# Moving four rings of buffers by a few words inside SBUF: start addresses modulo 256 bytes in a TensorE-bound MoE kernel

## The chip, the cores and the metric

The kernel runs on one NeuronCore of a Trainium2 chip. The metric is the device time of one execution in microseconds (us). Five engines work beside each other and meet at semaphores: PE (TensorE, the matrix engine), DVE (VectorE), ACT (ScalarE), POOL (GpSimd) and SP (SyncE, which here only issues DMAs). They share SBUF, an on-chip memory of 128 partitions; an address below is always a byte offset inside a partition, the same in all 128. Matmul results land in PSUM.

A matmul on PE has two operands in SBUF. The *stationary* one (128 columns here) is loaded into the array by a LDWEIGHTS instruction; the *moving* one (448 or 256 columns here, called rows below[...]) then streams through it. In the profile "PEld" is the row of weight loads and "PE" the row of matmuls; a weight load can run while the matmul before it still streams. The *pitch* of a matmul is the time from its start to the start of the next matmul.

## The reference

One layer: cross-attention over 16 batches of 112 tokens (width 256, context of 375), then a mixture of 8 experts of which every token uses all, weighted by a router.

```python
x = x + xattn(layernorm(x), ctx_1024, Wq, bq, Wk, bk, Wv, bv)
# ffn, on hidden = layernorm(x), 16*112 = 1792 tokens, H = 256, F = 1024, E = 8
g = einsum('bsh,ehf->ebsf', hidden, w_gate)
u = einsum('bsh,ehf->ebsf', hidden, w_up)
h = silu(g) * u
expert_out = einsum('ebsf,efh->ebsh', h, w_down)
out = einsum('ebsh,bse->bsh', expert_out, cw)     # cw: product of two softmaxes, normalised
x = x + out
```

All inputs and outputs are float32.

## The kernel before

**Attention first.** Up to about 110 us the attention of the 16 batches runs, a generator per batch advanced by a hand-written order (`tick`), and its tail is mixed into the first two steps of the expert loop. Its matrix products are plain float32, except the output projection `ps_o` (L337), which multiplies split operands like the expert loop does.

**The expert loop.** `steps` (L435) counts 8 experts x 2 halves of the tokens x 4 blocks of 256 hidden units x {gate, up} = 128 steps. Every float32 operand is split into a high and a low part of type float32r, and a product is three matmuls: high x high, high x low, low x high (`PASSES`, L79). One step computes a 256 x 256 by 256 x 896 product by Strassen-Winograd's seven products instead of eight (`PROD`, L20). `prod` (L568) does one of the seven: three matmuls, stationary a 128-column slice of the split gate or up weights `w` (high or low), moving a 448-column tile `xs_hi` or `xs_lo` of the prepared tokens (L573). A step has 21 of these.

Between them `fill` (L589) interleaves the down projection of earlier steps. `down_group` (L526) is three matmuls into a PSUM accumulator `pd` (L539): stationary a 128-token slice of `hhi` (twice) or `hlo` (once), the two parts of silu(gate) x up, moving the 256-column split down weights `wd` (high, low, high). There are 2688 matmuls of L573 and 2688 of L539, and the order on PE is the one written out in `step` (L646): runs of three, six or nine matmuls of the one kind and then of the other.

**What the other engines do for it.** ACT makes the high parts (`load_hi` L481, `load_d` L490, `keep_hidden` L625), POOL subtracts to make the low parts of the weights (`load_lo` L486, L491), DVE combines the seven products out of PSUM and makes `hlo` (L626, L633). SP issues the DMAs of raw weights.

**Where the buffers lie.** Buffers that rotate come from one pool, `fpool`, through one helper, `buf(tag, ...)` (L103); a tag is a ring with the number of buffers in `BUFS` (L101). The pool lays its rings one behind the other, in the order in which their tags first appear in the program, each buffer after the last: `y`, `w`, `d` (down weights), `rawd`, `hhi`, `hlo`, `tt`, `s`, `v1`, `raw`. Behind them comes the pool of small tiles. The tiles of another pool, the constants (`xs_hi`, `xs_lo`, the accumulators), lie ahead. As built, every buffer of `fpool` has a size that is a multiple of 256 bytes, so a whole ring has one remainder modulo 256. These are the remainders at which tiles begin:

| tiles | role on PE | bytes of a buffer | begins at, modulo 256 |
|---|---|---|---|
| `xs_hi`, `xs_lo` | moving, L573 | 1792 | 192 |
| `w` (gate and up, high and low) | stationary, L573 | 7168 | 64 |
| `d` (`wd`, high and low) | moving, L539 | 4096 | 64 |
| `hhi`, `hlo` | stationary, L539 | 3584 | 64 |
| `rawd`, `tt`, `s`, `v1`, `raw` | not read by PE in the loop | 2048 or 1792 | 64 |

A slice inside these (a product's weights, 128 tokens, the low half) is a multiple of 512 bytes from the tile's start, so it has the tile's remainder.

Of the kernel before, what the change touches and what calls it, by code (L numbers as in the profile page):

```python
# [8 lines left out]
F32 = mybir.dt.float32  # L9
# [22 lines left out]
def kernel(  # L32
# [18 lines left out]
    P = 128  # L51
# [20 lines left out]
    fpool = ctx.enter_context(tc.tile_pool(name="ffn", bufs=2))  # L72
# [27 lines left out]

    BUFS = {"w": 8, "d": 4, "hhi": 4, "hlo": 4, "s": 11, "v1": 2, "raw": 3, "rawd": 2, "tt": 2, "y": 3}  # L101

    def buf(tag, shape, name, dtype=F32):  # L103
        return fpool.tile(shape, dtype, tag=tag, name=name, bufs=BUFS[tag])

    zero = buf("y", [P, 256], "zero")
    nc.vector.memset(zero, 0.0)
    zero = zero.bitcast(mybir.dt.bfloat16)
# [16 lines left out]

    WF = 2 * 7 * P
    wide = [buf("w", [P, WF], f"wide{i}") for i in range(7)]
    qk_b = [wide[0][:, i * KC * GT : (i + 1) * KC * GT] for i in range(2)]
    late = [wide[i] for i in (3, 1, 2)]
# [4 lines left out]
    x1T = [wide[5 + h].rearrange("p (k t) -> p k t", k=KC) for h in range(NH)]  # L134

    wn = buf("d", [P, 2, KC, D], "wn")
    wT = buf("d", [P, 2, KC, D], "wT")
    wv_b = buf("d", [P, 2, KC, D], "wv_b", FR)
# [768 lines left out]
```

## Time and profile before

| | |
|---|---|
| median of 3 runs | 1004.95 us (1004.35 to 1006.24) |
| the profiled execution, its own time | 1002.7 us |
| its span, first to last instruction | 1000.9 us |
| granted TensorE clock, mean | 0.988 |
| DVE busy | 802.8 us (80%) |
| ACT busy | 496.4 us (50%) |
| POOL busy | 419.0 us (42%) |
| DMA queue of SP | 37.76 MB, 13.1% of 16 engines' span |

The profiled execution took 1.8 us more than its span, and 2.3 us less than the median of the runs. "Busy" is time in which at least one instruction of the engine is recorded. A matmul's recorded duration reaches over the start of the next ones, because they are pipelined and their ends are modelled; the distances between starts tell the rate at which PE moves.

### The profile page before, as it was taken

The numbers are of one execution on the slowest core, as the hardware profiler recorded it, in microseconds if no ns is written. First come the engines' busy times: TensorE is split into PE (matmuls) and PEld (weight loads), VectorE is DVE, ScalarE is ACT, GpSimd is POOL, SyncE is SP. The second block draws the span as 40 slices with busy tenths as digits, with TensorE's granted clock in tenths as the row PEclk, the third lists the DMA queues.
The fourth block names the chain that finished last, engine by engine and source line by source line (L and its number), as shares of the span: only waits on it lengthen the run. The fifth ranks groups of instructions, "written<-read, shape, count | busy, mean of one in ns | idle before, by whom it ended". The sixth has DMA issues, their size and how long they took to land.

```text
span 1000.9 us, 16367 instructions
## 1 busy us (share of the span) xinstructions
PE 980.1 (98%) x6052; PEld 911.3 (91%) x6052; DVE 802.8 (80%) x1529; ACT 496.4 (50%) x1036; POOL 419.0 (42%) x548
## 2 busy tenths in 40 slices
PE   8989889999999999999999999999999999999998
PEld 4868779999999999999999999999999999999998
DVE  5886668888878888878887887888887888788786
ACT  4555655445535554445544553555444544455342
POOL 2352765344605552356324460555235632455000
PEclk9999979999999999999999999999999999999999
DMA  9710111001100110011100110011001110010011
GB/s 216 213 30 16 53 32 53 16 28 44 53 1 23 43 43 22 12 42 37 39 11 22 44 54 1 22 44 43 22 11 43 44 32 11 22 43 2 1 37 38
DMA packets 36736, 39.06 MB, mean 39 GB/s; under 512 B 3552, under 2 KB 34656, under 8 KB 36656
## 3 DMA queue, kind: packets, MB, share of 16 engines
q1 hardware_dynamic: 36384, 37.76, 13.1%
q8 instruction: 47, 0.77, 0.3%
q10 hardware_dynamic: 272, 0.26, 0.1%
q14 instruction: 33, 0.27, 0.1%
HBM read 34.34 MB, written 1.84 MB: 36 GB/s over the span
## 4 chain that ended last, share of the span: by engine, by line
PE 93%; DVE 2%; DMA 2%; ACT 1%; POOL 1%; issue 0%; SPq 0%; DVEq 0%
PE pd L539 32%; PE pC L573 16%; PE pA L573 16%; PE pB L573 15%; PE pE L573 8%; PE ps_s L300 2%; PE ps_aT L327 1%; DMA wide<-in_x_dram 1%; PE ps_o L337 1%; PE ps_qk L271 1%; PE ps_lg L401 1%; DMA ctx<-in_ctx_dram 1%; PE ps_cT L293 1%; PE ps_pT L318 1%; ACT xs_hi L375 0%; POOL w L486 0%
## 5 line engine op out<-in xcount | busy, mean ns | idle before, releaser
L539 PE MATMUL pd<-wd,hhi 128*128 128x256 f32 x1792 | 338.6, 280 | 0.0
L539 PEld LDWEIGHTS pd<-wd,hhi 128*128 128x128 f32 x1792 | 310.1, 189 | 15.8
L539 PE MATMUL pd<-wd,hlo 128*128 128x256 f32 x896 | 251.9, 281 | 0.0
L573 PE MATMUL pC<-xs_hi,w 128*128 128x448 f32 x512 | 189.3, 370 | 0.8 <-DVE s_3c L702 0.8
L573 PE MATMUL pA<-xs_hi,w 128*128 128x448 f32 x512 | 188.6, 368 | 0.5 <-ACT v L674 0.4
L573 PE MATMUL pB<-xs_hi,w 128*128 128x448 f32 x512 | 187.9, 367 | 0.0
L539 PEld LDWEIGHTS pd<-wd,hlo 128*128 128x128 f32 x896 | 169.7, 189 | 0.2 <-DVE hlo L626 0.2
L556 POOL TENSOR_TENSOR acc<-acc,y 128x256 f32<-128x256 f32 x45 | 36.1, 831 | 248.4 <-ACT y L555 248.4
L486 POOL TENSOR_TENSOR w<-raw,w 128x384 fp32r<-128x384 f32 x64 | 73.0, 1141 | 136.8 <-ACT w L481 136.8
L674 ACT COPY v<-pA 128x448 f32<-128x448 f32 x128 | 68.1, 532 | 91.2 <-PE pA L573 91.2
L573 PEld LDWEIGHTS pC<-xs_hi,w 128*128 128x128 f32 x512 | 96.8, 189 | 10.0 <-DVE s_3c L702 1.1
L573 PEld LDWEIGHTS pA<-xs_hi,w 128*128 128x128 f32 x512 | 96.8, 189 | 6.0 <-ACT v L674 1.1
L573 PEld LDWEIGHTS pB<-xs_hi,w 128*128 128x128 f32 x512 | 97.2, 190 | 5.5
L573 PE MATMUL pC<-xs_lo,w 128*128 128x448 f32 x256 | 94.1, 368 | 0.0
L573 PE MATMUL pA<-xs_lo,w 128*128 128x448 f32 x256 | 94.1, 368 | 0.0
L573 PE MATMUL pE<-xs_hi,w 128*128 128x448 f32 x256 | 93.7, 366 | 0.0
L573 PE MATMUL pB<-xs_lo,w 128*128 128x448 f32 x256 | 93.3, 364 | 0.0
L486 POOL TENSOR_TENSOR w<-tt,w 128x512 fp32r<-128x512 f32 x64 | 82.9, 1296 | 2.6
L491 POOL TENSOR_TENSOR wd<-rawd,wd 128x512 fp32r<-128x512 f32 x32 | 41.8, 1307 | 72.7 <-ACT wd L490 72.7
L573 PEld LDWEIGHTS pE<-xs_hi,w 128*128 128x128 f32 x256 | 48.2, 188 | 3.9
L573 PEld LDWEIGHTS pB<-xs_lo,w 128*128 128x128 f32 x256 | 48.9, 191 | 1.9
L573 PEld LDWEIGHTS pC<-xs_lo,w 128*128 128x128 f32 x256 | 48.3, 189 | 2.3
(1779 smaller groups left out, 1884.4 us busy)
## 6 DMA issues: line engine op xcount, KB each, us to landing
raw<-in_L_ffn_w_gate_dram SPq DMA_DIRECT2D x32, 256.0 KB, 3.7
raw<-in_L_ffn_w_up_dram SPq DMA_DIRECT2D x32, 256.0 KB, 2.7
rawd<-in_L_ffn_w_down_dram SPq DMA_DIRECT2D x32, 256.0 KB, 2.8
ctx<-in_ctx_dram SPq DMA_DIRECT2D x13, 336.0 KB, 7.3
wide<-in_x_dram SPq DMA_DIRECT2D x4, 448.0 KB, 4.7
out_dram<-acc SPq DMA_DIRECT2D x6, 256.0 KB, 2.2
wide<-in_ctx_dram SPq DMA_DIRECT2D x3, 336.0 KB, 7.0
ctx<-in_ctx_dram SPq DMA_DIRECT2D x13, 39.0 KB
```

The lines of the kernel that those rows point to most:

```text
L271: nc.tensor.matmul(ps, m_sb[:, k, m * P : (m + 1) * P], xnT[:, k, :], start=(k == 0), stop=(k == KC - 1),)
L293: nc.tensor.transpose(ps[:, c * KT : (c + 1) * KT], ct[:, c, k * P : (k + 1) * P], ident[:KT, :KT])
L300: nc.tensor.matmul(sc, qkT[g][:, k, i * TQ : (i + 1) * TQ], ctT[k], start=(k == 0), stop=(k == KC - 1),)
L318: nc.tensor.transpose(ps[:, c, :], p[:, c * KT : (c + 1) * KT], ident[:TQ, :TQ])
L327: nc.tensor.matmul(ps[:, k, :], ct[:, c, k * P : (k + 1) * P], pT[:, c, :], start=(c == 0), stop=(c == NK - 1),)
L337: nc.tensor.matmul(po, aT[:, a, k, :], (wv_hi, wv_lo)[w][:, k, :], start=(k == 0 and s == 0), stop=(k == KC - 1 and s == 2),)
L486: nc.gpsimd.tensor_sub(wts[k][1][:, d], w, f(wts[k][0][:, d]))
L491: nc.gpsimd.tensor_sub(t[:, 1], rawds[q], f(t[:, 0]))
L539: nc.tensor.matmul(pd, hs[a][:, t * P : (t + 1) * P], wds[q][w][:, fi, :], start=(opening and s == 0), stop=(last and s == 2), skip_group_ ...
L556: nc.gpsimd.tensor_add(acc[tt], acc[tt], y)
L573: nc.tensor.matmul(ps, w_[w][:, wi, :], (xs_hi, xs_lo)[a][h][xi], start=(start and s == 0), stop=(stop and s == 2), skip_group_check=True,)
L674: nc.scalar.copy(v1, pa)
```

## The change

`buf` gets a second table. When one of four tags appears for the first time, a small tile of its own (16 or 32 float32 words, 64 or 128 bytes) is taken from the same pool just ahead of the ring. Nothing ever writes or reads these tiles.

```diff
     BUFS = {"w": 8, "d": 4, "hhi": 4, "hlo": 4, "s": 11, "v1": 2, "raw": 3, "rawd": 2, "tt": 2, "y": 3}
 
+
+    AHEAD = {"w": 16, "d": 32, "hhi": 16, "hlo": 32}
+
     def buf(tag, shape, name, dtype=F32):
+        if tag in AHEAD:
+            fpool.tile([P, AHEAD.pop(tag)], F32, tag=f"ahead_{tag}", name=f"ahead_{tag}", bufs=1)
         return fpool.tile(shape, dtype, tag=tag, name=name, bufs=BUFS[tag])
```

As built, this moves everything behind `y`:

| tiles | modulo 256 before | after |
|---|---|---|
| `xs_hi`, `xs_lo`, `y`, accumulators | 192, 192, 64, 192 | the same |
| `w` | 64 | 128 |
| `d`, and `rawd` behind it | 64 | 0 |
| `hhi` | 64 | 64 |
| `hlo`, and `tt`, `s`, `v1`, `raw` behind it | 64 | 192 |

In all 384 bytes per partition are taken. The instructions of each of the five engines, their order and the semaphores that they wait for are the same as before; only start addresses differ.

## The prediction

> **What bounds the kernel now.** I read the page's busy table first, then the stages, then single starts on PE.
>
> ```profile
> span 1000.9 us, 16367 instructions
> ...
> PE 980.1 (98%) x6052; PEld 911.3 (91%) x6052; DVE 802.8 (80%) x1529; ACT 496.4 (50%) x1036; POOL 419.0 (42%) x548
> ...
> PE 93%; DVE 2%; DMA 2%; ACT 1%; POOL 1%; issue 0%; SPq 0%; DVEq 0%
> ```
>
> PE carries 93% of the chain that ended last. The waits of PE, cut to the steady part of the loop (150 to 985 us), hold one row of 0.8 us, and the stages view of a part of it shows PE without a gap:
>
> ```profile
> PE pC L573 <- DVE s_3c L702: 0.8, 1, 0.8
> ```
>
> ```profile
> 500.00:900.00 400.00, 400.00 (x2490) 379.75 (x2490) 329.82 (x563) 200.21 (x395) 171.33 (x212) 1.00 0.10 29
> ```
>
> The columns are length, then busy time and count of PE, PEld, DVE, ACT, POOL, then clock, DMA share, GB/s. So the pitch of the matmuls is the time. By line the same stretch has 1248 matmuls of L539 and 1242 of L573, that is 1248 x 256 + 1242 x 448 = 875,904 rows.
>
> Now the price of a row. PE ran at half clock around 137 us; its timeline (start, recorded duration) there, then at full clock:
>
> ```profile
> 136.14 0.57 PE L573 MATMUL pA<-xs_lo,w 128*128 128x448 f32 x1
> ...
> 138.75 0.57 PE L573 MATMUL pC<-xs_hi,w 128*128 128x448 f32 x1
> ```
>
> ```profile
> 503.04 0.36 PE L573 MATMUL pA<-xs_hi,w 128*128 128x448 f32 x1
> 503.24 0.36 PE L573 MATMUL pA<-xs_lo,w 128*128 128x448 f32 x1
> 503.44 0.36 PE L573 MATMUL pA<-xs_hi,w 128*128 128x448 f32 x1
> 503.65 0.36 PE L573 MATMUL pB<-xs_hi,w 128*128 128x448 f32 x1
> ```
>
> ```profile
> 506.79 0.40 PE L539 MATMUL pd<-wd,hhi 128*128 128x256 f32 x2
> 507.03 0.28 PE L539 MATMUL pd<-wd,hlo 128*128 128x256 f32 x1
> 507.15 0.40 PE L539 MATMUL pd<-wd,hhi 128*128 128x256 f32 x2
> 507.39 0.28 PE L539 MATMUL pd<-wd,hlo 128*128 128x256 f32 x1
> 507.51 0.37 PE L573 MATMUL pB<-xs_hi,w 128*128 128x448 f32 x1
> ```
>
> At half clock seven matmuls of L573 take 2.61 us, 373 ns each: 0.833 ns a row and nothing over. A row at full clock is then 0.4165 ns, 186.6 ns for 448 and 106.6 for 256. At full clock L573 has a pitch of 203 (three in 0.61 us) and a long run of L539 of 120 (six in 0.72 us). From all single starts I get a mean of 203.1 for L573 (stalls over 230 ns left out) and 118.0 for L539. So 16.5 and 11.4 ns a matmul are neither rows nor waits, 35 us of the 400 above (875,904 x 0.4165 = 364.8), and they are gone when the rows come at half the rate. The other engines do not make them either: from step to step the same place of the loop repeats its pitch within 1 ns, though in gate steps ACT takes silu and in up steps DVE multiplies. The plain float32 matmuls of the attention, which take two clocks a row (375 rows in 315 ns, 312.5 by the count), have nearly none. I read the excess as two streams of PE meeting in SBUF: the moving rows at full rate, and the next weights, whose load starts 2 to 3 ns after each matmul and is recorded with 188 ns. The change alters where those two streams start, and nothing else.
>
> **What the Trainium skill says.** "TensorE: Matmul & The Clock Gate", section Back-to-back issue gap, prices an isolated matmul at N / 2.4 + 2.5 ns: 189.2 for 448, 109.2 for 256. The trace is 14 and 9 ns above. The same page, Step-by-step, says of the two read ports of PE that loading the next weights "doesn't steal SBUF read bandwidth from the running matmul"; the excess that is there at full clock and not at half speaks against that here. "SBUF — State Buffer", Who interferes with whom, has no contention but that of DVE with GpSimd, and Operand start alignment treats start addresses as a matter of legality and says that its runs "timed nothing". No page gives a price for a remainder modulo 256: it has to be bounded.
>
> **The change part by part.**
>
> *Instructions.* None is added, removed or moved, on no engine and no queue, SP's DMAs included. Set-up cost 0.
>
> *Which offsets change.* Take the start of the weights being loaded minus the start of the rows streaming, modulo 256, for each pair of neighbours on PE.
> - L573 behind L573 (2190 pairs): 64 - 192 = 128 before, 128 - 192 = 192 after.
> - L539 behind L539 (2190): 0 before. After: 64 for a load of `hhi` (two in each group of three, but for those that start a run: 1294), 192 for a load of `hlo` (896).
> - L539 behind L573 (498): 128 before and after. L573 behind L539 (497): 0 before, 128 after.
>
> *What an offset costs.* The loop shows only 128 (excess 16.5) and 0 (11.4; 13.3 in long runs). The one other place with split operands is `ps_o`, whose rows start at 64 and whose weights (112 columns) start at 192, 0, 0 and 128 in its second to fifth gap: offsets 128, 192, 192, 64. Over the 13 batches that ran at full clock these gaps average 115.5, 117.6, 114.6 and 117.5 ns: 116.3, or 9.7 over the rows. Weights of 112 columns are 7/8 of 128, so a full load would cost 11.1. The plain float32 scores `ps_s` have all four offsets and 314 to 315 ns at each once they run, so at half the row rate no offset costs anything.
>
> *L539.* From 11.4 to 11.1: 0.3 x 2190 = 0.7 us gained. Bounds: all excess above the skill's gap gone, 8.8 x 2190 = 19 us gained; L573's excess instead of its own, 5.1 x 2190 = 11 us lost.
>
> *L573.* If the offset is what makes it dearer, it falls from 16.5 to 11.1: 5.4 x 2190 = 11.8 us gained. If its length is, nothing. `ps_o` at offset 128 is no dearer than at the others, which speaks for length; but the same load of 128 columns should meet the same number of rows in both kinds, which speaks for offset. I take two thirds, 7.9 us. Bounds: 13.9 x 2190 = 30 us gained, and 5.4 x 2190 = 12 us lost if 192 is as much worse than 128 as 128 is than the rest.
>
> *The turns.* L539 to L573 goes from 0 to 128: at worst 5.1 x 497 = 2.5 us lost, taken as 0, as a turn at 128 in the other direction shows no jump of its own.
>
> *Other engines.* DVE, ACT and POOL read and write at new remainders. DVE's combinations (L679, L700, L702, L714, L724) take 602 to 624 ns each with all their SBUF operands at one remainder, and those with two SBUF inputs start at 610 too, so I see no price that could go or come. Cover if there were one: DVE is busy 83% of the steady part, and PE waits for it 0.8 us. Gone, that cover would cost at one place only, the wait of pC for DVE, where a few steps already start over 100 ns late (some 2 us in all). What comes due next if PE gets faster is the same wait: DVE has 400 - 330 = 70 us spare in 400, so a few per cent do not reach it.
>
> *Sum.* 0.7 + 7.9 = 8.6 us less than the profiled 1002.7: 994.1. Its distance to the median (2.3) added: 996.4, say 996.
>
> **The rivals.**
> - *Offsets do not matter, only the two rates do* (1005). For it: `ps_o` with mixed offsets costs per column of weights what L539 costs with offset 0. Against it: [...] no run of the trace holds another offset long enough.
> - *The new offsets keep the two streams in step* (slower). Rows advance at up to twice the speed of a load, so a stream that starts 64 bytes apart can run into the other and stay with it. Place: the long runs of L539, now at 64 and 192. Price: L539 at L573's excess, 5.1 x 2190 = 11 us, L573 unchanged: 1016. It decides once the mean pitch of L539 goes over 118 + 7.9 / 2.19 = 121.6 ns. For it: L573 pays 16.5 with its start apart, L539 11.4 with the same start. Against: `ps_o`.
> - *The excess mostly goes* (970): half to two thirds of the pool above the skill's gap, 30 + 19 us. For it: nothing in the records but the size of the pool.
> - *The free words do not shift what PE reads*: excluded, as the tiles' addresses are moved as the title says.
>
> **How the numbers follow.** Forecast, a gain of some 3 to 20 us: 0.42. Excess mostly gone: 0.10. No effect: 0.17. Slower: 0.31. About 0.2% (2 us) is what a measurement of this kernel tells from no change; that is 0.37 ns a matmul, so "same" holds only where offsets have no effect or the two kinds cancel. Faster 0.52, same 0.17, slower 0.31. The likeliest case alone spans 985 to 1002; the range over the cases, leaving some 0.1 at each end, is 971 to 1017.
>
> **What would show it.** Right: L573's pitch in the timeline falls from 203 to about 199 and L539's long runs stay at 117 to 120, with clock 1.00 and the wait table as it is. Offsets without effect: 203 and 120 again. The slower rival: long runs of L539 at 123 or more. I would be wrong in kind if the time moved while these two pitches stood still, for then another engine's accesses would have carried it; and wrong in part if L539 took the gain and L573 none.

## The result, and the profile after

| | before | after |
|---|---|---|
| median (lowest to highest) of 19 runs each, us | 1004.89 (1002.06 to 1006.63) | 1001.23 (999.53 to 1003.28) |
| ratio, with its 95% interval | | 0.9969 (0.9959 to 0.9978) |
| the profiled execution, span in us | 1000.9 | 1000.8 |
| loop, step 10 to step 126, in those two traces, us | 783.8 | 781.6 |

The change is worth 0.31% (0.22 to 0.41), some 3 us. The forecast was 0.9%. The two profiled executions are no guide to that: their spans agree because after's attention part, ahead of the loop, took longer in this one execution (the loop begins at 112.7 us instead of 110.2; in the traces of the kernels below that keep the whole layer it begins anywhere from 109.8 to 114.0). The same stretch of the loop is 2.2 us shorter.

The page of the kernel after, its busy table and the shares of its chain:

```profile
span 1000.8 us, 16367 instructions
...
PE 978.5 (98%) x6052; PEld 911.8 (91%) x6052; DVE 802.9 (80%) x1529; ACT 496.1 (50%) x1036; POOL 419.4 (42%) x548
...
PE 93%; DVE 2%; DMA 2%; ACT 1%; POOL 0%; issue 0%; SPq 0%; DVEq 0%
```

Its waits of PE in the steady part, 150 to 985 us (total, times, longest):

```profile
PE pC L578 <- DVE s_3c L707: 0.8, 1, 0.8
```

And 400 us of the loop (length, busy time and count of PE, PEld, DVE, ACT, POOL, clock, DMA share, GB/s):

```profile
500.00:900.00 400.00, 400.00 (x2497) 380.87 (x2496) 330.36 (x565) 199.78 (x394) 170.87 (x212) 1.00 0.10 29
```

Same instructions, same chain, same single wait of 0.8 us, full clock. PE gets through 2497 matmuls in the 400 us instead of 2490: it moves at a shorter pitch, by 0.3%, and these views show no other change. The pitch shows in the timeline of PE in the kernel after (start, recorded duration; the lines are the earlier ones plus 5, so L544 was L539 and L578 was L573):

```profile
500.10 0.36 PE L578 MATMUL pA<-xs_hi,w 128*128 128x448 f32 x1
500.30 0.36 PE L578 MATMUL pA<-xs_lo,w 128*128 128x448 f32 x1
...
501.10 0.36 PE L578 MATMUL pE<-xs_hi,w 128*128 128x448 f32 x1
501.30 0.40 PE L544 MATMUL pd<-wd,hhi 128*128 128x256 f32 x2
...
502.24 0.28 PE L544 MATMUL pd<-wd,hlo 128*128 128x256 f32 x1
502.36 0.37 PE L578 MATMUL pB<-xs_hi,w 128*128 128x448 f32 x1
...
502.98 0.40 PE L544 MATMUL pd<-wd,hhi 128*128 128x256 f32 x2
```

The six matmuls of L573 from 500.10 to 501.30 take 200 ns each. The nine of L539 from 501.30 to 502.36 take 118. The three of L573 that follow them take 207 (502.36 to 502.98): the same instruction with operands at the same remainders is 7 ns dearer here than 2 us earlier. That last reading is the one that the forecast had no place for.

All later numbers are mean pitches, worked out as here from single starts in each trace, from 150 us on, with stalls over 230 ns left out. A turn is the place where a run of one kind of matmul ends and a run of the other begins. A pitch belongs to a matmul and to the load for the next one, so there are four kinds of neighbours. In the table the offset (next weights' start minus running rows' start, modulo 256) stands in brackets. "Sum" is each difference from before, times the 2190, 497, 498 and 2190 such pairs, in us; "measured" is the ratio's distance from 1 times 1005 us. Each ratio is to the kernel before, run on the same chip in the same sitting. Lines are named as in the kernel before. The nine kernels below "after" belong to the experiments.

| kernel | L539 to L539 | L539 to L573 | L573 to L539 | L573 to L573 | sum | measured |
|---|---|---|---|---|---|---|
| before | 117.8 (0) | 118.6 (0) | 205.3 (128) | 202.5 (128) | | |
| after | 117.2 (64), 119.2 (192) | 117.4 (128) | 205.2 (128) | 200.9 (192) | -3.6 | -3.1 |
| w_only | 118.2 (0) | 117.9 (64) | 202.8 (128) | 202.1 (192) | -1.8 | -1.8 |
| d_only | 115.9 (64) | 116.6 (64) | 202.8 (128) | 203.7 (128) | -3.9 | -4.9 |
| rest_only | 117.8 (0) | 118.6 (0) | 205.2 (128) | 202.6 (128) | 0.0 | -0.2 |
| no_hlo | 114.8 (64) | 118.0 (128) | 204.1 (128) | 199.7 (192) | -13.7 | -12.2 |
| near | 118.2 (64) | 117.5 (64) | 199.8 (192) | 201.5 (192) | -4.8 | -3.2 |
| near96 | 117.5 (64) | 118.1 (224) | 200.6 (192) | 204.2 (96) | +0.4 | +0.4 |
| hlo_alone | 117.1 (64), 119.1 (192) | 117.6 (128) | 205.0 (128) | 201.0 (192) | -3.8 | -4.7 |
| turn0 | 116.0 (64) | 114.1 (0) | 201.2 (0) | 200.4 (192) | -12.9 | -12.3 |
| turn64 | 114.6 (64) | 114.8 (192) | 203.3 (64) | 200.0 (192) | -15.3 | -14.4 |

In every row the pitches account for the measured difference within 1.6 us, so what these kernels gain or lose is a matter of these four pitches.

### The profile page after: what moved, and what is told of

Same layout as the page of the kernel before. It is cut to its first block, busy times and chain, and to the rows that moved or that the text cites. A ratio compares the mean times of both kernels' runs of the same rounds, so it can differ in the third digit from the quotient of the medians.

```text
span 1000.8 us, 16367 instructions
## 1 busy us (share of the span) xinstructions
PE 978.5 (98%) x6052; PEld 911.8 (91%) x6052; DVE 802.9 (80%) x1529; ACT 496.1 (50%) x1036; POOL 419.4 (42%) x548
## 4 chain that ended last, share of the span: by engine, by line
PE 93%; DVE 2%; DMA 2%; ACT 1%; POOL 0%; issue 0%; SPq 0%; DVEq 0%
PE pd L544 32%; PE pC L578 16%; PE pA L578 15%; PE pB L578 15%; PE pE L578 8%; PE ps_s L305 2%; PE ps_aT L332 1%; PE ps_o L342 1%; DMA wide<-in_x_dram 1%; PE ps_qk L276 1%; PE ps_lg L406 1%; DMA ctx<-in_ctx_dram 1%; PE ps_cT L298 1%; PE ps_pT L323 0%; ACT xs_hi L380 0%; PE ps_x1T L369 0%
## 5 line engine op out<-in xcount | busy, mean ns | idle before, releaser
L544 PE MATMUL pd<-wd,hhi 128*128 128x256 f32 x1792 | 338.8, 280 | 0.0
L544 PEld LDWEIGHTS pd<-wd,hhi 128*128 128x128 f32 x1792 | 308.9, 188 | 14.1
L544 PE MATMUL pd<-wd,hlo 128*128 128x256 f32 x896 | 250.6, 280 | 0.0
L578 PE MATMUL pC<-xs_hi,w 128*128 128x448 f32 x512 | 189.7, 370 | 0.8 <-DVE s_3c L707 0.8
L578 PE MATMUL pB<-xs_hi,w 128*128 128x448 f32 x512 | 188.6, 368 | 0.0
L578 PE MATMUL pA<-xs_hi,w 128*128 128x448 f32 x512 | 187.4, 366 | 0.9 <-ACT v L679 0.4
L544 PEld LDWEIGHTS pd<-wd,hlo 128*128 128x128 f32 x896 | 169.3, 189 | 0.0
L578 PEld LDWEIGHTS pC<-xs_hi,w 128*128 128x128 f32 x512 | 96.8, 189 | 11.3 <-DVE s_3c L707 1.1
L578 PEld LDWEIGHTS pB<-xs_hi,w 128*128 128x128 f32 x512 | 97.1, 190 | 5.6
L578 PEld LDWEIGHTS pA<-xs_hi,w 128*128 128x128 f32 x512 | 96.6, 189 | 5.9 <-ACT v L679 1.0
L578 PE MATMUL pC<-xs_lo,w 128*128 128x448 f32 x256 | 93.6, 366 | 0.0
L578 PE MATMUL pE<-xs_hi,w 128*128 128x448 f32 x256 | 93.4, 365 | 0.0
L578 PE MATMUL pB<-xs_lo,w 128*128 128x448 f32 x256 | 93.1, 364 | 0.0
L578 PE MATMUL pA<-xs_lo,w 128*128 128x448 f32 x256 | 92.7, 362 | 0.0
L578 PEld LDWEIGHTS pE<-xs_hi,w 128*128 128x128 f32 x256 | 48.2, 188 | 3.2
L578 PEld LDWEIGHTS pC<-xs_lo,w 128*128 128x128 f32 x256 | 48.5, 189 | 1.5
L578 PEld LDWEIGHTS pB<-xs_lo,w 128*128 128x128 f32 x256 | 48.3, 189 | 1.7
```

The source lines that it names most:

```text
L544: nc.tensor.matmul(pd, hs[a][:, t * P : (t + 1) * P], wds[q][w][:, fi, :], start=(opening and s == 0), stop=(last and s == 2), skip_group_ ...
L578: nc.tensor.matmul(ps, w_[w][:, wi, :], (xs_hi, xs_lo)[a][h][xi], start=(start and s == 0), stop=(stop and s == 2), skip_group_check=True,)
```

## The experiments

The theory carried over from the forecast, A in the expectations, is that the excess is made by PE's own two streams of reads, the moving rows and the next weights, and that the offset between them sets its size. The expectations name the rivals.

### map_one: the price of an offset by itself

The layer is left out. PE runs 30 equal matmuls for each offset in steps of 16 bytes, at 448 and then 256 rows. ACT, DVE, POOL and the DMAs do nothing meanwhile.

```diff
+    N = 30
...
+    for n in (448, 256):
+        for o in range(0, 256, 16):
...
+            m0 = ROWS_AT // 4
+            w0 = (ROWS_AT + o) // 4 + 64
+            for i in range(N):
+                nc.tensor.matmul(
+                    ps[:, :n], wts[:, w0 : w0 + P], rows[:, m0 : m0 + n],
...
```

`ROWS_AT` is 0.

> All of the layer is left out: 24 warm-up matmuls, then for 448 and for 256 rows and for each offset of 0, 16, ... 240 bytes (start of the stationary columns minus start of the moving rows, modulo 256) 30 equal float32r matmuls with a load of 128 columns each, nothing beside them on any engine. Theory A, the moving rows and the next weights collide in SBUF and the remainder of the offset modulo 256 decides how often: the pitch differs by 2 ns or more between offsets, at 448 rows 128 is dearer than 192 (about 202.5 to 201), and at 256 rows 0, 64 and 192 lie within 2 ns of each other near 117 to 120. Rival B, the offset between PE's two streams costs nothing and the gain came from where other engines read and write: one pitch for all 16 offsets, to within 0.5 ns. Rival C, the excess is no matter of SBUF but a fixed price of a load: about 203 and 120 at every offset.

The timeline of PE (start, recorded duration; the letter at the end of a name counts the offset, a is 0, e is 64, i is 128, m is 192):

```profile
48.10 6.17 PE L44 MATMUL pl_g<-rows,wts 128*128 128x448 f32 x30
54.10 6.28 PE L44 MATMUL pl_h<-rows,wts 128*128 128x448 f32 x30
60.22 6.28 PE L44 MATMUL pl_i<-rows,wts 128*128 128x448 f32 x30
66.33 6.23 PE L44 MATMUL pl_j<-rows,wts 128*128 128x448 f32 x30
...
84.66 6.17 PE L44 MATMUL pl_m<-rows,wts 128*128 128x448 f32 x30
90.67 6.29 PE L44 MATMUL pl_n<-rows,wts 128*128 128x448 f32 x30
...
109.08 3.76 PE L44 MATMUL ps_a<-rows,wts 128*128 128x256 f32 x30
112.67 3.72 PE L44 MATMUL ps_b<-rows,wts 128*128 128x256 f32 x30
...
123.31 3.57 PE L44 MATMUL ps_e<-rows,wts 128*128 128x256 f32 x30
126.72 3.73 PE L44 MATMUL ps_f<-rows,wts 128*128 128x256 f32 x30
```

From one block's start to the next: 6.11 us at 128 (60.22 to 66.33) against 6.01 at 192; 3.59 us at 0 against 3.41 at 64. In single pitches, the mean of the last 15 of each block:

| offset | 0 | 32 | 64 | 96 | 128 | 160 | 192 | 224 |
|---|---|---|---|---|---|---|---|---|
| 448 rows, ns | 202.7 | 204.5 | 202.3 | 200.0 | 204.0 | 205.3 | 200.0 | 206.7 |
| 256 rows, ns | 120.0 | 118.1 | 113.3 | 118.7 | 120.0 | 120.2 | 117.7 | 116.7 |

So moving only the start of the weights changes the pitch, with PE alone: by up to 6.7 ns at 448 rows and 6.9 at 256. Rivals B and C fall with that. One part of A falls too: at 256 rows, 0, 64 and 192 were to lie within 2 ns and lie 6.7 apart. And no offset takes the excess away. At offset 0 it is 16.1 ns over the rows' 186.6 at 448 rows and 13.4 over 106.6 at 256 rows, and at each of the 16 offsets 448 rows pay more than 256.

### w_only, d_only, rest_only: the parts of the change

Only `w` moves to 128; only `d` (with `rawd`) moves to 0; or PE's four rings move by a whole 256 bytes, with `tt`, `s`, `v1` and `raw`, which PE does not read in the loop, shifted to 192.

```diff
-    AHEAD = {"w": 16, "d": 32, "hhi": 16, "hlo": 32}
+    AHEAD = {"w": 16, "d": 48}              # w_only
+    AHEAD = {"d": 48, "hhi": 16}            # d_only
+    AHEAD = {"w": 64, "tt": 32}             # rest_only
```

> Only the gate and up weights are moved, to 128; down weights, hhi, hlo and all behind them stay at 64. Theory A: the neighbours L573-L573 take the 200.9 ns of the kernel after (202.5 before), 1.6 x 2190 = 3.5 us off, L539-L539 keep 117.8, and L573 behind L539, now at offset 64 instead of 128, is open within 1 ns (0.5 us). About 0.3 to 0.4% faster, the whole gain of the change or a little more. Rival B: no change, ratio 1.000.

> Only the down weights (and the raw ones behind them) are moved, to 0; all else stays at 64. Offset of L539-L539 is 64 for all. Theory A: L573-L573 keep 202.5 ns; L539-L539 go from 117.8 to 117.2, which is what hhi has in the kernel after: 0.6 x 2190 = 1.3 us, 0.1% faster; if instead the run of one offset settles differently than the mix of 64 and 192, up to 2 ns either way. Rival B: no change.

> What PE reads in the expert loop keeps its remainders (the ring of gate and up weights and all behind it is pushed by 256 bytes); tt, s, v1 and raw alone begin at 192 instead of 64, as in the kernel after. Theory A: every place of the loop has the pitch of the kernel before to within 0.5 ns, ratio 1.000 within 0.1%. Rival B: it brings the gain, ratio 0.997.

The ratios are 0.9982 (0.9967 to 0.9997), 0.9951 (0.9932 to 0.9970) and 0.9998 (0.9987 to 1.0009). 400 us of rest_only, columns as above:

```profile
500.00:900.00 400.00, 400.00 (x2487) 379.69 (x2487) 329.38 (x562) 197.34 (x389) 169.18 (x209) 1.00 0.10 29
```

With `tt`, `s`, `v1` and `raw` where after has them and PE at its old offsets, all four pitches are before's, within 0.2 ns. Nothing of the result comes from what DVE, ACT and POOL read and write there. What they write into PE's own rings is not tested by this; loop_alone, below, does without it. The other two miss in opposite ways. w_only was to gain 0.3 to 0.4% and gains 0.18%: it puts L573 at offset 192, as after does, and gains 0.5 ns there, where after gained 1.6. d_only was to gain some 0.1% and gains 0.49%: it leaves L573 at 128, where it gets 1.1 ns dearer with nothing of its own moved, and finds its gain in L539 at 64, 1.9 ns. The parts do not add up as prices of offsets: the same offset is worth a different amount beside other neighbours.

### map_two: is the offset all there is?

The layer is left out. Blocks of 30 matmuls at offsets 0, 64, 128 and 192, at three pairs of places with the same offset modulo 256 ("base", "far", "off"), then with 512 rows, and with plain float32.

```diff
...
+        for n in (448, 256):
...
+            block(f"base{t}_{x}", n, 64, 64 + o + 256)
+            block(f"far{t}_{x}", n, 0, o + 1024)
+            block(f"off{t}_{x}", n, 512, 512 + o + 768)
+        block(f"big_{x}", 512, 0, o + 256)
+        block(f"plain_{x}", 256, 0, o + 256, 16, True)
```

> Again only matmuls, the layer left out. For offsets 0, 64, 128 and 192 and both row counts: base = rows start 64 bytes later than in map_one, weights with them; far = weights 1024 bytes from the rows plus the offset; off = rows start 512 later, weights 768 further. big = 512 rows; plain = 256 rows of plain float32 (two passes, two clocks a row). Theory A, only the difference of the two starts modulo 256 counts: base, far and off repeat map_one within 0.5 ns, that is 202.7, 202.4, 204.0, 200.1 at 448 rows and 120.0, 113.4, 120.2, 117.8 at 256; big shows differences of 1 to 5 ns over 213.3; plain lies at 213 to 216 a pass with less than 1 ns between offsets. Rival: absolute addresses or bits above 256 count, then base, far or off differ from map_one by 2 ns or more somewhere.

The timeline of PE at offset 64, 256 rows:

```profile
73.02 3.58 PE L42 MATMUL bases_b<-rows,wts 128*128 128x256 f32 x30
76.43 3.70 PE L42 MATMUL fars_b<-rows,wts 128*128 128x256 f32 x30
79.97 3.70 PE L42 MATMUL offs_b<-rows,wts 128*128 128x256 f32 x30
83.50 7.17 PE L42 MATMUL big_b<-rows,wts 128*128 128x512 f32 x30
```

One offset, two pitches: 3.41 us a block in the first place, 3.54 and 3.53 in the others, that is 113.3 against 117.8 ns over the last 15. At 448 rows the same happens at 128 (206.7 against 204.0); at 0, 64 and 192 the three places agree within 0.1 ns, as at the other offsets of 256 rows. So theory A's 0.5 ns holds at six of the eight pairs of offset and length, and at two the rival's 2 ns or more is there. A settled block repeats a short cycle of pitches: 209, 196, 204, 211, 200 in the one case, 207, 207, 206 in the other. With 512 rows the four offsets cost 226.7, 233.1, 233.6 and 228.9 ns. Plain float32, at two clocks a row, costs 215.8 to 215.9 at all four. The offset modulo 256 is thus most of the story, but it leaves at least two values open. Whether the place or what ran before chose between them, this kernel cannot say.

### no_hlo: the change without its last tile

```diff
-    AHEAD = {"w": 16, "d": 32, "hhi": 16, "hlo": 32}
+    AHEAD = {"w": 16, "d": 32, "hhi": 16}
```

`hlo`, and all that lies behind it, stays at 64, so every load of L539 is at offset 64, the cheap one of the map at 256 rows.

> The kernel after, but hlo and the rings behind it stay at 64: every load of hhi and hlo starts 64 behind the down weights' rows, gate and up weights are at 128 as in the kernel after. Theory A: L539-L539 at 115.9 as in d_only (118.1 in the kernel after) = 2.2 x 2190 = 4.8 us less than after, L573-L573 about 200.9 to 202: steps 10 to 126 in 776.5 to 780 us (after 781.6, d_only 780.5), ratio to before 0.990 to 0.995. Rival D, hlo at 192 is part of the gain (DVE writes and reads hlo and s there): slower than the kernel after, over 0.997.

Median 991.39 us, ratio 0.9879 (0.9860 to 0.9899), a larger gain than the 0.990 to 0.995 expected. A window and the timeline of PE in no_hlo (its lines are before's plus 4):

```profile
500.00:900.00 400.00, 400.00 (x2523) 381.26 (x2522) 335.67 (x574) 202.81 (x400) 178.62 (x223) 1.00 0.10 29
```

```profile
501.90 0.40 PE L543 MATMUL pd<-wd,hhi 128*128 128x256 f32 x2
...
502.24 0.39 PE L543 MATMUL pd<-wd,hhi 128*128 128x256 f32 x2
...
502.93 0.36 PE L577 MATMUL pB<-xs_hi,w 128*128 128x448 f32 x1
503.13 0.36 PE L577 MATMUL pB<-xs_lo,w 128*128 128x448 f32 x1
503.33 0.36 PE L577 MATMUL pB<-xs_hi,w 128*128 128x448 f32 x1
503.53 0.40 PE L543 MATMUL pd<-wd,hhi 128*128 128x256 f32 x2
```

Six matmuls of L539 in 0.69 us are 115 each, and the three of L573 behind the run take 200 where after's took 207. One of the four free tiles, the one ahead of `hlo`, gives back three quarters of what the other three gain: 9 us of 12.2. L539 is 3.2 ns a matmul better without it (7.0 us over 2190), and L573 as well, by 1.3 ns (2.8 us), although its own offset is 192 in both kernels.

### near, near96: the cheap offsets chosen from the map

Both keep L539 at 64. near keeps L573 at 192 too, and of the offsets only those at the turns differ from no_hlo; near96 puts L573 at 96, the cheapest of the map.

```diff
-    AHEAD = {"w": 16, "d": 32, "hhi": 16, "hlo": 32}
+    AHEAD = {"w": 16, "d": 48, "hhi": 16}   # near
+    AHEAD = {"w": 56, "d": 8, "hhi": 16}    # near96
```

> A version that the map suggests: gate and up weights at 128, down weights at 64, hhi and hlo at 128. All pairs of neighbours then have one of the two cheap offsets: L573-L573 192, L539-L539 64, L539 behind L573 192 (128 before and after), L573 behind L539 64. Theory A with the map's steady pitches: 200.1 and 113.4 where runs settle; with 202.5 and 117.8 before that would be 2.4 x 2190 + 4.4 x 2190 = 14.9 us, and since the runs of three to nine do not all settle I expect half to all of it: ratio 0.985 to 0.993. Rival: the turns decide and the order of runs undoes it, ratio over 0.995.

> As near, but gate and up weights at 32, so that L573-L573 have offset 96, the other cheap place of map_one at 448 rows, reached from the first matmul on (200 in every one); L573 behind L539 is at 224. Theory A: L573-L573 at 200 to 201, L539-L539 as in near: within 0.2% of near. If offset 96 is cheap only in long runs: slower than near by 0.3% or more.

Both missed: 0.9968 (0.9956 to 0.9980) and 1.0004 (0.9992 to 1.0016). For near, the rival's figure of over 0.995 came true. (Two of its 15 executions took 996.7 and 997.5 us, the others 1000.0 to 1002.3; why is not known.) In near96, L573 at the map's cheapest offset has 204.2, and in the run of nine of the up step 205 to 207. The timeline of PE in near, the same place as above:

```profile
501.21 0.40 PE L543 MATMUL pd<-wd,hhi 128*128 128x256 f32 x2
...
501.56 0.40 PE L543 MATMUL pd<-wd,hhi 128*128 128x256 f32 x2
...
502.27 0.37 PE L577 MATMUL pB<-xs_hi,w 128*128 128x448 f32 x1
```

Six of L539 from 501.56 take 0.71 us, 118 each, at the same offset 64 that gave 115 in no_hlo. And L573 to L573 has 201.5 against 199.7 with `xs` and `w` at the very same addresses in both kernels. What differs for those pairs is what PE ran before them. For L539 the places of the operands differ too, but not between d_only and no_hlo: there `wd`, `hhi` and `hlo` lie at the very same addresses, only `w` has moved, and L539 to L539 has 115.9 in the one and 114.8 in the other. So a run can have more than one pitch at the same addresses, and what precedes it has a say in which. A map of steady blocks cannot choose between such versions.

### loop_alone: PE by itself, in the loop's order

The layer is left out; PE alone runs the 42 matmuls of an up step, six times over for each of four sets of remainders, with small tiles at other addresses.

```diff
+    RUNS = ((9, 3), (6, 9), (3, 6), (3, 3))       # L573's, L539's
+    SETS = (("before", 192, 64, 64, 64, 64), ("after", 192, 128, 0, 64, 192),
+            ("nohlo", 192, 128, 0, 64, 64), ("near", 192, 128, 64, 128, 128))
```

> The layer is left out: only PE's matmuls of an up step, in the loop's run lengths (9 of 448 rows, 3 of 256, 6, 9, 3, 6, 3, 3), six times for each of four sets of start remainders (xs, w, wd, hhi, hlo): before 192, 64, 64, 64, 64; after 192, 128, 0, 64, 192; nohlo 192, 128, 0, 64, 64; near 192, 128, 64, 128, 128. No other engine works beside them. Theory A, PE's own two streams make the whole of it: the 42 matmuls of one turn of the pattern take what they take in the full kernels' steady part: 6736, 6715, 6638 and 6705 ns, each within 20 ns. If other engines' accesses have a part in it: off by more, and the distances between the four sets shrink.

The timeline of PE, for the set of after:

```profile
56.87 0.76 PE L59 MATMUL pl_after<-xs,w 128*128 128x448 f32 x3
57.47 0.40 PE L59 MATMUL ps_after<-wd,hhi 128*128 128x256 f32 x2
...
65.87 1.96 PE L59 MATMUL pl_after<-xs,w 128*128 128x448 f32 x9
...
70.29 0.78 PE L59 MATMUL pl_after<-xs,w 128*128 128x448 f32 x3
70.91 0.40 PE L59 MATMUL ps_after<-wd,hhi 128*128 128x256 f32 x2
...
72.59 1.96 PE L59 MATMUL pl_after<-xs,w 128*128 128x448 f32 x9
```

and of no_hlo:

```profile
99.36 1.96 PE L59 MATMUL pl_nohlo<-xs,w 128*128 128x448 f32 x9
105.99 1.96 PE L59 MATMUL pl_nohlo<-xs,w 128*128 128x448 f32 x9
```

A cycle of after takes 6.72 us here, one of no_hlo 6.63. The medians over the up steps of the full kernels, from 150 us on and from the first L573 of a step to that of the next, agree with the settled cycles (the expectation's figures for them were up to 5 ns off):

| 42 matmuls, ns | before | after | no_hlo | near |
|---|---|---|---|---|
| full kernel | 6740 | 6713 | 6633 | 6705 |
| PE alone | 6740 | 6713 | 6633 | 6701 to 6705 |

PE alone makes the whole effect, the differences between versions included: 27 ns from before to after, times 128 steps, is 3.5 us. The pair of lines at 56.87 against the pair at 70.29 shows the dependence on history directly: the same three matmuls on the same addresses took 0.60 us in the first cycle, 27 matmuls behind the change from another set, and 0.62 in the third, although those 27 are the same in both.

### hlo_alone, turn0, turn64: the cause narrowed, and the best version

hlo_alone returns `tt`, `s`, `v1` and `raw`, which lie behind `hlo`, to the remainder they have in no_hlo, so that of all remainders only that of `hlo`, 192, differs from no_hlo. turn0 and turn64 keep no_hlo's offsets inside the runs, 64 and 192, and change the two turns to 0 and 0, and to 192 and 64.

```diff
-    AHEAD = {"w": 16, "d": 32, "hhi": 16, "hlo": 32}
+    AHEAD = {"w": 16, "d": 32, "hhi": 16, "hlo": 32, "tt": 32}   # hlo_alone
+    AHEAD = {"w": 16, "hhi": 16}                                 # turn0
+    AHEAD = {"w": 16, "d": 16, "hhi": 16}                        # turn64
```

> The kernel after with tt, s, v1 and raw put back to 64, so that against no_hlo only hlo is moved, from 64 to 192. Theory A: the loads of hlo at 192 undo the settled state of the down projection, L539-L539 at 118.1 and L573-L573 at 200.9 as in the kernel after, ratio 0.996 to 0.998. Rival D', it is what DVE and ACT read and write behind hlo that gave the time back: then it stays near no_hlo, 0.986 to 0.990.

> Same offsets inside runs as no_hlo and near (L573-L573 192, L539-L539 64), other turns: 0 from L573 to L539 and 0 back (gate and up weights 128, down weights 128, hhi and hlo 192). Theory E, a run keeps the state in which the turn puts it, so turns alone are worth up to 1%: L539-L539 pitch settles at 113.3 or at 117.8 and the ratio is near 0.988 or near 0.997, not between by averaging. If turns only cost themselves (995 of them), it lies within 2 ns x 995 = 2 us of no_hlo.

> As turn0, with turns of 64 from L573 to L539 and 192 back (gate and up weights 128, down weights 192, hhi and hlo 0). Theory E: again one of the two levels, 0.988 or 0.997; which one is open. If turns only cost themselves: within 2 us of no_hlo.

Windows of hlo_alone, turn0 and turn64, in this order:

```profile
500.00:900.00 400.00, 400.00 (x2497) 381.08 (x2496) 330.76 (x566) 200.98 (x397) 174.07 (x215) 1.00 0.10 29
```

```profile
500.00:900.00 400.00, 400.00 (x2520) 381.88 (x2519) 335.88 (x572) 202.54 (x399) 179.14 (x223) 1.00 0.09 29
```

```profile
500.00:900.00 400.00, 400.00 (x2529) 381.14 (x2528) 337.00 (x575) 203.81 (x403) 178.91 (x223) 1.00 0.09 29
```

hlo_alone is at 0.9953 (0.9937 to 0.9968), with after's count of 2497 and after's pitches within 0.2 ns: the loads of `hlo` at 192 undo no_hlo by themselves. turn0 has 0.9878 (0.9862 to 0.9895), turn64 0.9857 (0.9841 to 0.9874), 990.86 us. With near, turn0 and turn64 are three versions with the same offsets in their runs as no_hlo. Their L539 runs stand between 114.6 and 118.2 ns, their L573 runs between 200.0 and 201.5. In the up step's run of nine L539, no_hlo, turn0 and turn64 come down to 113 ns and near stays at 117 to 119: about the two values that map_two has for this offset. That is what theory E says, and near's 9 us are far over the 2 us of turns that cost only themselves; turn0 and turn64 by themselves lie near no_hlo, as both would have it. turn64 has the lowest ratio of all that ran, 1.4% under before; the intervals of no_hlo and turn0 overlap with its own, so these three are not told apart. Even there DVE has 400 - 337 = 63 us to spare in 400.

## Why the prediction was right or wrong

- *PE's pitch is the time, and nothing else bounds it.* Right. The table of waits is unchanged, and the pitches alone account for every version.
- *The excess is two streams of PE meeting in SBUF.* Supported, not proved: the offset between moving rows and weights changes it with PE alone (map_one, loop_alone), and plain float32 at two clocks a row shows no such change (map_two). The sentence that the forecast quoted from the Trainium skill, "TensorE: Matmul & The Clock Gate", Step-by-step, that loading the next weights takes no read bandwidth from the running matmul, is hard to square with that. That they collide in SBUF is argued from this; where and how is not shown.
- *L573: 5.4 ns x 2190 x two thirds = 7.9 us.* This is the step that failed in size. It measured 202.54 to 200.93, 1.6 ns x 2190 = 3.5 us. Its premise was that at a good offset L573's excess would fall to `ps_o`'s 11.1 ns. The map says otherwise: at every offset 448 rows cost at least 13.4 ns over their rows, and the steady difference between 128 and 192 is 4.0 ns. The argument that the same load should meet the same number of rows in both kinds does not fit the map, as 448 rows pay more than 256 at every one of its offsets. Of the 4.0, less than half arrived: before's runs, broken up by L539, stood at 202.5 and not at the map's 204.0, and after's, which reach 200 in the up step's runs of six and nine, stand at 204 to 205 in its runs of three and so at 200.9 in the mean.
- *L539: 0.3 ns x 2190 = 0.7 us gained.* Wrong in sign, small in size: 117.79 to 118.06 in the mean, 0.6 us lost. The step took one price from `ps_o` for offsets 64 and 192 together. There is no one price: 119.2 for the loads of `hlo` at 192, and with all loads at 64 it is 114.8 in no_hlo, but 118.2 in near. The chance of a much larger gain lay here, and the fourth free tile spent it.
- *Turns taken as 0.* The pairs at the turns themselves moved by 0.6 us, L539 to L573, from 118.6 to 117.4, and by 0.1 in the other direction; so the term was nearly right. The step was wrong in another way: it counted a turn by its own pitch. Where the offsets inside the runs are the same and those at the turns differ, no_hlo, near, turn0 and turn64 lie up to 11 us apart, and from no_hlo to near the runs lose some 11 us (7.3 in L539, 4.1 in L573) while the turns themselves gain 2.4. The pitch of a pair is not a function of its own offset alone.
- *Other engines: nothing.* Right: rest_only has 0.9998, and loop_alone gives the steps of the full kernels with no other engine at work.
- *The rivals.* "Offsets do not matter" falls with the map. "The new offsets keep the streams in step" was not reached: L539 would have needed 121.6 ns and had 118.1, yet its part at 192 did rise, from 118.0 to 119.2, and hlo_alone shows that these loads are what holds the gain down. Whether by two streams that keep in step is not shown. "The excess mostly goes" did not come about in any version; turn64 removes 14 us of the forecast's pool of 49.

By its own sum: 3.5 (L573) + 0.6 and 0.1 (turns) - 0.6 (L539) = 3.6 us, measured 3.1 (2.2 to 4.1). The direction was forecast for the right reason, L573 at 192, but with some luck: by `w` alone at its new remainder (w_only) L573 to L573 gains 0.5 ns, and it takes the new neighbours, which the forecast gave no part in this, to make it 1.6. The size was under half.

What stays open: why one offset has two pitches, and which order of turns leads to which. loop_alone reproduces each set, but no rule found here tells the pitch of a new set before it runs; near and near96 were two failed attempts.

## What to carry to other kernels

Where PE runs back to back at full clock on split float32 operands, the start addresses of moving rows and weights relative to each other, modulo 256, are a tuning knob that costs no instruction: here 1.4% over the whole kernel. (That 256 is the period was taken from the start; map_two bears it out at six of eight pairs and was not made to try other periods.) Price it with a small kernel that runs PE alone in the loop's own order of matmuls, since steady blocks of one kind gave misleading prices and such a small kernel came within 4 ns in 6700. Try the parts of such a change one at a time, because one tile of four gave back three quarters of what the other three gained.

## What the runs showed of the hardware that was not expected

- Offsets matter in steps down to 16 bytes and follow no simple order: at 448 rows, 0, 16, 32 and 48 bytes gave 202.7, 206.7, 204.5 and 202.3 ns, and the cheapest were 96 and 192 (200.0 both). Yet L573 at offset 96 had 205 to 207 in the run of nine of near96's up step. At 256 rows it was 64 (113.3), with 116.6 to 120.2 elsewhere.
- An excess over the rows stays at every offset: 6.7 ns at best for 256 rows, 13.4 for 448, and for 512 rows, at the best of four offsets, 226.7 less 213.2 (512 x 0.4165), 13.5. So the excess does not simply grow with the rows: at offset 0 it is 13.4, 16.1 and 13.5 for 256, 448 and 512. The Trainium skill, "TensorE: Matmul & The Clock Gate", Back-to-back issue gap, prices an isolated matmul at 2.5 ns over its rows; no block of split operands here reached that, while 256 rows of plain float32, at two clocks a row, had 215.8 less 213.2, 2.6.
- A run of matmuls keeps a pitch that depends on what ran ahead of it: 0.60 or 0.62 us for the same three instructions in loop_alone, 199.7 or 201.5 ns for L573 at equal addresses in no_hlo and near.
- The Trainium skill, "SBUF — State Buffer", Operand start alignment, treats start addresses as a question of what is allowed. Here all starts were allowed, and they moved the kernel from 1005.3 to 990.9 us (turn64).
